# Layer 0 without full-height products: sums by turns and a small product, projection in halves, queries' products moved into layer 1

## Chip, cores and metric

The kernel runs on one NeuronCore of one Trainium2 chip. The metric is the device time of one execution in microseconds. Everything is float32. Before the change, three runs give 3160.32, 3160.87 and 3160.97 us, median 3160.87 us.

## What is computed

The input is x of shape (4, 128, 64, 64): four batches, 128 channels, 4096 positions. Three parts follow one another.

```python
# layer 0, on the group-normalised input
vg = sigmoid(conv_bn(x, Wvg, svg, bvg)); v, gate = split(vg, 2)
q = conv_bn(x, Wq, sq, bq) * 64**-0.5        # 64 channels
k = conv_bn(x, Wk, sk, bk)                   # 64 channels
attn = softmax(einsum('bdn,bdm->bnm', q, k))
out = einsum('bcm,bnm->bcn', v, attn) * gate
x = x + conv_bn(out, Wp, sp, bp)             # the projection
# layer 1, on tokens t = x turned to (batch, position, channel)
h = layernorm(t)
q = einsum('bsd,de->bse', h, W)              # queries are the keys too
t = t + einsum('bst,btd->bsd', softmax(einsum('bsd,btd->bst', q, q)), h)
# a recurrent layer over the positions
Wx = batchnorm(layernorm(t) @ W.T)
t = t + scan(lambda y, wx: sigmoid(wx + y @ V.T), Wx)
```

## The kernel before

**Tiling.** For each batch the kernel runs `layer0` (L368) and then `layer1` (L435). The 4096 positions make 8 blocks of 512 (`QB`, `NB`), each of 4 tiles of 128 (`NQ`).

**Layer 0.** `attention` (L178) takes the blocks in order. For each block it goes through 16 pairs of key tiles. A pair has two scores products (L200), each with a contraction over 64 channels only, one on rows 0 to 63 and one on rows 64 to 127 of the array. They write `ps`, a tile of two PSUM banks from a pool with two buffers (tag "s"). ScalarE takes the exponential of both at once (L202), VectorE adds it to `acc` (L209), which gathers the sums of the softmax for each of the 128 key rows, and two pairs later `weigh` (L376) multiplies it with the values: four products, again each over 64 rows, into two accumulators `o`. When the last pair of a block has been weighed, `finish` (L389) adds the two accumulators, applies the gate to get `og`, and appends six steps to the queue `pending`: `sums`, `projection`, `nothing`, `tokens`, `nothing`, `queries` (L430). The loop takes one step from it at each second pair (L217). The last block's steps are left for layer 1.

**The steps.** `sums` calls `denominators` (L222): VectorE folds the two halves of `acc`, and four products of 128x128 with a column of ones (L227, tile `md`) sum over the key rows, which leaves one sum per position, with the positions on the partitions. `projection` is one 128x128x512 product (L409, tile `mt`), over all 128 rows. `tokens` (L412) scales the projected values, adds the input, stores the tokens and normalises them into `h`. `queries` (L422) is one 128x128x512 product (L424, tile `mq`) that ScalarE copies into `qt` (L427). All three products go to PSUM pool `ps_m`, which has one buffer.

**Turns.** `move` (L235) turns a 128x512 tile from channels on partitions to positions on partitions, or back. VectorE's transpose turns blocks of 32x32 in place (L241), one DMA writes the result to DRAM (L244) and four read it back so that the blocks change places (L246). It is used for the input (in `sums`), for the projected values and for `h`. All DMAs concerned are issued by SP.

**Layer 1.** It takes block 6 first, then 7, then 5 down to 0 (L560). Scores between two blocks serve both: `e` as it is (`direct`, L460), and turned by VectorE (L584) and sixteen DMAs `tt<-dd` (L605) for the other block (`reversed_products`, L471). All products here go over 128 rows. In each step of the inner loop one item of `pending` is taken, or, if it is empty, one of `ahead`, which prepares the next batch (L598 to L601).

**Order.** The program text gives the order in which work is put out. The framework then orders each engine's instructions by what it takes to be ready, so an instruction on VectorE, SP or GpSimd can stand at another place than in the text: the input of a block is loaded and turned during the block before.

Of the kernel before, what the change touches and what calls it, by code (L numbers as in the profile page):

```python
# [18 lines left out]
P = 128  # L19
B, C, N = 4, 128, 4096  # L20
DQ = 64
SCALE = DQ ** -0.5
GROUP = 4
NT = N // P
# [5 lines left out]
QB = 512  # L30
# [18 lines left out]
@with_exitstack  # L49
def conv_attn_hybrid_kernel(  # L50
    ctx: ExitStack,
    tc: tile.TileContext,
    x: bass.AP,
    wts: bass.AP,
    cols: bass.AP,
    rows: bass.AP,
    out: bass.AP,
):
    nc = tc.nc

# [35 lines left out]
    nc.gpsimd.affine_select(  # L96
        out=gview, in_=gview, compare_op=ALU.is_ge, fill=0.0, base=GROUP - 1,
        pattern=[[GROUP, P // GROUP], [0, GROUP]], channel_multiplier=-1,
    )
    mhalf = const.tile([P, NQ], F32, name="mhalf")  # L100
    nc.gpsimd.memset(mhalf, -0.5)
    ones = const.tile([P, 1], F32, name="ones")
    nc.gpsimd.memset(ones, 1.0)
    shift = const.tile([P, 1], F32, name="shift")
    nc.gpsimd.memset(shift, -SHIFT)

    nc.vector.tensor_mul(w_v, w_v, bc[:, 0, :])
    nc.vector.tensor_mul(w_p, w_p, bc[:, 2, :])
    w_vs, w_ps = w_v, w_p

    par2 = const.tile([P, 2], F32, name="par2")
    nc.vector.tensor_scalar(par2, par[:, SG : BG + 1], 0.5, None, ALU.mult)
# [7 lines left out]
    fast(  # L120
        tc, x, out, t_d, t2_d, wxs_d, turn_d,
        dict(qk=w[:, DQ : DQ + P], vs=w_vs, g=w_g, ps=w_ps, a=w_a, f=w_f, vt=v_t),
        col, par, par2, bpc, bc, ident, gavg, ones, shift, inv_sqrt, par_ok,
    )
# [16 lines left out]


def fast(
    tc, x, out, t_d, t2_d, wxs_d, turn_d, wt, col, par, par2, bpc, bc, ident, gavg, ones,
    shift, inv_sqrt, par_ok,
):
    nc = tc.nc
    keep_ctx = ExitStack()
# [4 lines left out]
    with ExitStack() as st:  # L153
# [19 lines left out]
        def flush(until=None):  # L173

            while pending and until not in done:
                pending.popleft()()
# [42 lines left out]
            while fifo:  # L219
                pop()  # L220

        def denominators(acc, at, rinv):  # L222

            nc.vector.tensor_tensor(acc[:, 0, :], acc[:, 0, :], acc[:, 1, :], ALU.add)
            m = ps_m.tile([P, NQ], F32, tag="m", name="md")
            for j in range(NQ):
                nc.tensor.matmul(  # L227
                    m[:, j : j + 1], lhsT=acc[:, 0, bass.ts(j, P)], rhs=ones,
                    start=True, stop=True,
                )  # L230
            den = den_all[:, at : at + NQ]
            nc.vector.tensor_copy(den, m)
            nc.vector.reciprocal(rinv, den)

        def move(blocks, dst):  # L235

# [131 lines left out]
        def layer0(b, gate, q, k, v, need):  # L368
# [20 lines left out]
            def finish(n, o, acc):  # L389
                cs, ts = bass.ts(n, QB), bass.ts(n, NQ)  # L390
                og = work.tile([P, QB], F32, tag="og", name="og")
                nc.scalar.copy(og, o[1])
                nc.vector.tensor_tensor(og, o[0], og, ALU.add)
                nc.vector.tensor_tensor(og, og, gate[:, cs], ALU.mult)
                rinv = stat.tile([P, NQ], F32, tag="rinv", name="rinv")
                xb = work.tile([P, QB], F32, tag="xb", name="xb")
                t = work.tile([P, 4, NQ, 32], F32, tag="t", name="t", bufs=2)
                yt = work.tile([P, 4, NQ, 32], F32, tag="h2", name="yt")
                ht = work.tile([P, 4, NQ, 32], F32, tag="th", name="ht")
                nc.sync.dma_start(xb, x[b, :, cs])  # L400
                nc.gpsimd.tensor_scalar(xb, xb, bpc, None, ALU.add)  # L401

                def sums():
                    denominators(acc, b * NT + n * NQ, rinv)
                    move(xb.rearrange("c (j f k) -> c j f k", j=NQ, f=4), t)

                def projection():
                    m = ps_m.tile([P, QB], F32, tag="m", name="mt")
                    nc.tensor.matmul(m, lhsT=wt["ps"], rhs=og, start=True, stop=True)  # L409
                    move(m.rearrange("c (j f k) -> c j f k", j=NQ, f=4), yt)  # L410

                def tokens():  # L412
                    for j in range(NQ):
                        nc.vector.scalar_tensor_tensor(
                            t[:, :, j, :], yt[:, :, j, :], rinv[:, j : j + 1], t[:, :, j, :],
                            ALU.mult, ALU.add,
                        )
                    nc.sync.dma_start(t_d[b, n], t)
                    layernorm(tiles(t), quarters(h[:, ts, :]))
                    move(h[:, ts, :].rearrange("q j (p i) -> q j p i", p=4), ht)  # L420

                def queries():  # L422
                    m = ps_m.tile([P, QB], F32, tag="m", name="mq")
                    nc.tensor.matmul(  # L424
                        m, lhsT=wt["a"], rhs=ht.rearrange("c f j k -> c j f k"), start=True, stop=True
                    )
                    nc.scalar.copy(qt[:, cs], m)  # L427
                    done.add((b, n))

                pending.extend([sums, projection, nothing, tokens, nothing, queries])  # L430

            attention(score_mm, None, SCALE, weigh, finish, need)
            return h, qt
# [1 line left out]
        def layer1(b, h, qt):  # L435
# [12 lines left out]
            n_turned = 0  # L448
            parts = [0] * NB
            begun = set()  # L450

            def order(n):


                return [0, 1] if b == B - 1 and n == 0 else list(range(n, -1, -1))
# [104 lines left out]
            for n in [NB - 2, NB - 1] + list(range(NB - 3, -1, -1)):  # L560
                o = None
                flush((b, n))
                for a in order(n):
                    if turns(n, a):
                        d = dd[:, n_turned % 2]
# [2 lines left out]
                    for i in range(2):  # L568
# [18 lines left out]
                                )  # L587
                        if o is None:
                            o = ps_o.tile([P, QB], F32, tag="o", name="o")
                        fifo.append((n, a, i, e, o))  # L590
                        clock += 1
                        if len(fifo) > LAG:
# [556 lines left out]
```

## Time and profile before

Stages, from windows of the trace (us of busy time in each window):

| Stage | Window | Length | TensorE | VectorE | ScalarE |
|---|---|---|---|---|---|
| start | 0 to 25.9 | 25.9 | 7.9 | 14.9 | 4.1 |
| batch 0, layer 0 | 25.9 to 408.4 | 382.5 | 382.3 | 222.0 | 152.9 |
| batch 0, layer 1 | 408.4 to 794.6 | 386.2 | 381.2 | 218.7 | 129.3 |
| batch 1, layer 0 | 794.6 to 1162.6 | 368.0 | 368.0 | 214.8 | 140.8 |
| batch 1, layer 1 | 1162.6 to 1548.8 | 386.2 | 381.2 | 218.7 | 129.3 |
| batch 2, layer 0 | 1548.8 to 1916.8 | 368.0 | 368.0 | 214.7 | 140.8 |
| batch 2, layer 1 | 1916.8 to 2303.1 | 386.3 | 381.3 | 218.7 | 129.3 |
| batch 3, layer 0 | 2303.1 to 2671.0 | 367.9 | 367.9 | 214.7 | 140.9 |
| batch 3, layer 1 | 2671.0 to 3040.0 | 369.0 | 360.4 | 182.7 | 112.9 |
| its end, recurrent layer | 3040.0 to 3157.6 | 117.6 | 73.4 | 72.4 | 47.9 |

TensorE is the engine that is hardly ever idle; the others are busy for about a third to three fifths of each attention stage. The groups that the change concerns, from the page and the groups by shape:

| Line | What | Count | Mean of one, ns |
|---|---|---|---|
| L200 | scores, 64x512, TensorE | 2048 records | 602 |
| L383 | weighing, 64x512, TensorE | 4096 records | 589 |
| L227 | sums, 128x1, TensorE | 256 records | 251 |
| L409 | projection, 128x512, TensorE | 64 records | 638 |
| L424 | queries, 128x512, TensorE | 64 records | 639 |
| L202 | exponential, 128x1024, ScalarE | 512 | 1024 |
| L427 | copy of the queries, 128x512, ScalarE | 32 | 586 |
| L209 | accumulation of the sums, 128x1024, VectorE | 448 | 1220 |
| L224 | folding the sums, 128x512, VectorE | 32 | 692 |
| L232 | copy of the sums, 128x4, VectorE | 32 | 162 |
| L241 | turn of 128x512, VectorE | 96 | 702 to 718 |

A matmul in this type leaves two records, and [...]records overlap. What a product costs is read better from the distance between the starts of its neighbours, or from the chain of waits, than from the mean of a record.

### The profile page before, as it was taken

Reading aid. Unit: us, or ns where it says so; the run is one execution under the profiler, and the core shown is the slowest. Engines: PE = TensorE matmul, PEld = TensorE weight load, DVE = VectorE, ACT = ScalarE, POOL = GpSimd, SP = SyncE. Lnnn points to the kernel's source line nnn. Section 1 sums busy time; section 2 is a strip of 40 time slices with the busy share of each in tenths; the row PEclk is TensorE's granted clock in tenths of the full one; section 3 lists DMA queues with packets and bytes.
Section 4 is the critical chain, followed back from the end, with each engine's and each line's share of the span. In section 5 each row is a group of like instructions: output and inputs, shape, how many; then the busy total and the mean of one; then the engine's idle time right before and its main releaser. Section 6 shows DMA issues by size and latency. Waiting matters only on the chain.

```text
span 3157.6 us, 32263 instructions
## 1 busy us (share of the span) xinstructions
PE 3071.5 (97%) x10770; PEld 1374.8 (44%) x10770; DVE 1792.3 (57%) x2964; ACT 1128.2 (36%) x1986; POOL 141.4 (4%) x183
## 2 busy tenths in 40 slices
PE   7999999999999999999999999999999999999976
PEld 3444444444444444444444444444444444444433
DVE  6555556555555555655555555555555655454546
ACT  3433333333333333333333333333333333223324
POOL 0000000000000000000000000000000000000000
PEclk9999999999999999999999999999999999999988
DMA  1111133333111123334211113333321112443324
GB/s 50 37 44 54 54 100 93 92 90 92 48 50 51 54 70 91 96 87 98 70 54 51 54 45 98 93 93 93 88 53 54 54 48 72 136 105 89 98 87 169
DMA packets 233167, 241.14 MB, mean 76 GB/s; under 512 B 88480, under 2 KB 144288, under 8 KB 231968
## 3 DMA queue, kind: packets, MB, share of 16 engines
q1 hardware_dynamic: 231984, 238.18, 27.2%
q8 instruction: 89, 1.46, 0.2%
q10 hardware_dynamic: 1008, 0.79, 0.1%
q14 instruction: 86, 0.70, 0.1%
HBM read 65.80 MB, written 56.62 MB: 39 GB/s over the span
## 4 chain that ended last, share of the span: by engine, by line
PE 91%; DVE 4%; POOL 1%; DMA 1%; SPq 1%; issue 1%; ACT 1%; ACTq 0%; DVEq 0%; POOLq 0%
PE o L383 28%; PE ps L200 15%; PE o L463 14%; PE ps L573 13%; PE ot L476 12%; PE mt L409 1%; PE mq L424 1%; PE mw L544 1%; PE md L227 1%; PE mp L315 1%; PE ps_r L719 1%; PE mh L539 1%; POOL rstd L117 1%; DVE t1b L521 1%; PE mp L350 1%
## 5 line engine op out<-in xcount | busy, mean ns | idle before, releaser
L383 PE MATMUL o<-e,nxt 64*128 64x512 f32 x4096 | 963.8, 589 | 0.0
L202 ACT ACTIVATE e<-ps 128x1024 f32<-128x1024 f32 x512 | 521.2, 1024 | 742.7 <-PE ps L200 738.1
L209 DVE TENSOR_TENSOR acc<-acc,e 128x1024 f32<-128x1024 f32 x448 | 546.4, 1220 | 387.9 <-ACT e L202 376.6
L579 ACT ACTIVATE e<-ps,shift 128x512 f32<-128x512 f32 x580 | 394.0, 684 | 776.4 <-PE ps L573 486.2
L383 PEld LDWEIGHTS o<-e,nxt 64*128 64x128 f32 x4096 | 398.9, 187 | 482.4 <-issue 474.6
L573 PE MATMUL ps<-qt 128*128 128x512 f32 x1160 | 550.4, 595 | 3.0 <-ACT e L579 3.0
L200 PE MATMUL ps<-nxt 64*128 64x512 f32 x2048 | 540.9, 602 | 1.2 <-DVE nxt L327 0.9
L463 PE MATMUL o<-e,h 128*128 128x512 f32 x1160 | 537.0, 592 | 0.0
L476 PE MATMUL ot<-tt,h 128*128 128x512 f32 x888 | 401.5, 595 | 5.3 <-DMA tt<-dd 5.3
L584 DVE STREAM_TRANSPOSE dd<-e 128x512 f32<-128x512 f32 x444 | 286.1, 685 | 110.8 <-ACT e L579 57.3
L463 PEld LDWEIGHTS o<-e,h 128*128 128x128 f32 x1160 | 218.4, 190 | 262.1 <-issue 261.2
L573 PEld LDWEIGHTS ps<-qt 128*128 128x128 f32 x1160 | 213.2, 191 | 244.4 <-issue 224.2
L200 PEld LDWEIGHTS ps<-nxt 64*128 64x128 f32 x2048 | 189.5, 186 | 248.0 <-issue 162.7
L476 PEld LDWEIGHTS ot<-tt,h 128*128 128x128 f32 x888 | 168.3, 191 | 217.1 <-issue 212.4
L481 DVE TENSOR_REDUCE slots<-tt 128x4 f32<-128x2048 f32 x111 | 250.6, 2258 | 11.3 <-DMA tt<-dd 11.2
L490 DVE TENSOR_TENSOR oacc<-oacc,ot 128x512 f32<-128x512 f32 x87 | 59.3, 682 | 209.5 <-PE ot L476 209.5
L116 POOL TENSOR_SCALAR rstd<-mv 128x4 f32<-128x4 f32 x64 | 14.6, 228 | 2519.5 <-DVE mv L257 2519.5
L579 ACT ACTIVATION_READ_ACCUMULATOR e<-ps,shift 128x1 f32 x580 | 113.9, 196 | 0.0
L401 POOL TENSOR_SCALAR xb<-xb,bpc 128x512 f32<-128x512 f32 x32 | 54.3, 1698 | 318.0 <-DMA xb<-in_x_dram 285.2
L117 POOL TENSOR_TENSOR rstd<-rstd,mhalf 128x4 f32<-128x4 f32 x64 | 66.4, 1038 | 5.3
L719 PE MATMUL ps_r<-y,w 128*128 128x256 f32 x168 | 54.4, 443 | 9.8 <-ACT y L716 7.8
L260 DVE TENSOR_SCALAR h<-t,mv,rstd 128x128 f32<-128x128 f32 x128 | 35.7, 343 | 45.3 <-POOL rstd L117 45.3
(124 smaller groups left out, 1411.8 us busy)
## 6 DMA issues: line engine op xcount, KB each, us to landing
tt<-dd SPq DMA_DIRECT2D x1776, 64.0 KB, 2.0
turn_d<-d SPq DMA_DIRECT2D x96, 256.0 KB, 2.0
t_d<-t SPq DMA_DIRECT2D x64, 256.0 KB, 2.0
nxt<-in_x_dram SPq DMA_DIRECT2D x16, 512.0 KB, 5.8
xb<-in_x_dram SPq DMA_DIRECT2D x32, 256.0 KB, 2.9
t<-turn_d SPq DMA_DIRECT2D x128, 64.0 KB, 2.0
yt<-turn_d SPq DMA_DIRECT2D x128, 64.0 KB, 1.9
ht<-turn_d SPq DMA_DIRECT2D x128, 64.0 KB, 2.0
```

The costliest lines, as they stand in the source:

```text
L117: nc.gpsimd.tensor_tensor(dst, dst, mhalf[:, :n], ALU.pow)
L200: nc.tensor.matmul(ps[:, h, :], lhsT=lhsT, rhs=rhs, start=True, stop=True)
L202: nc.scalar.activation(e, ps, AF.Exp, scale=scale)
L209: nc.vector.tensor_tensor(acc, acc, e, ALU.add)
L383: nc.tensor.matmul(o[r], lhsT=v[rs, p + h * PAIRS, :], rhs=e[rs, h, :], start=(p == 0 and h == 0), stop=(p == PAIRS - 1 and h == 1),)
L463: nc.tensor.matmul(o, lhsT=h[:, NQ * a + 2 * i + half, :], rhs=e[:, half, :], start=(a == order(n)[0] and i == 0 and half == 0), stop=(a = ...
L476: nc.tensor.matmul(ot, lhsT=h[:, NQ * n + j, :], rhs=t[:, :, j, :, :].rearrange("q p k j -> q k p j"), start=(j == 0), stop=(j == NQ - 1),)
L481: nc.vector.tensor_reduce(slots[:, bass.ts(n, NQ), a], t.rearrange("q p b k j -> q b p (k j)"), AX.XY, ALU.add,)
L573: nc.tensor.matmul(ps[:, half, :], lhsT=qt[:, bass.ts(at, P)], rhs=qt[:, bass.ts(n, QB)], start=True, stop=True,)
L579: nc.scalar.activation(e[:, half, :], ps[:, half, :], AF.Exp, bias=shift, accum_out=slots[:, at, n : n + 1],)
L584: nc.vector.transpose(d.rearrange("q f b k j -> q k b f j")[:, 2 * i + half], e[:, half, :].rearrange("q (b f j) -> q b f j", b=NQ, f=NQ),)
L719: nc.tensor.matmul(bank(k, s), lhsT=wt["vt"], rhs=before, start=False, stop=True, skip_group_check=True,)
```

## The change

The denominators, the projection and the queries of layer 0 are computed in another way or at another place; the result is meant to be the same.

- **Sums.** `sums` still folds the halves of `acc`, but then VectorE turns the 32x32 blocks of the folded half into the other half of `acc` and adds up each row of a block (512 to 16 columns, tile `sub`). A new step `denominators` multiplies `sub` with a constant matrix `quart`, in two products of 64 rows each (`halves`), which adds the four groups of 32 partitions. VectorE then adds the two partial results, keeps for each partition the column of its own group (`own`, a mask) and adds that up.
- **Projection.** One product over 128 rows becomes two over 64 rows each, through the same `halves`. ScalarE copies one partial result, VectorE adds the other, and the turn reads the sum from SBUF.
- **Buffers.** `halves` takes its PSUM tile from the pool of the scores (tag "s", two buffers), not from `ps_m`.
- **Queries.** `tokens` now turns `h` straight into its place in `qt`, and the block counts as done there. The product is made in layer 1, in the pass of block 6: for block 6 ahead of the first scores, for block a-1 in the first half of key block a, for block 7 in the last half of key block 0. The result replaces the turned `h` in `qt`.
- **Queue.** The six steps are `sums`, `nothing`, `denominators`, `projection`, `nothing`, `tokens`.
- Two small constants, `quart` and `own`, are built at the start by VectorE.

```diff
+        def halves(lhsT, rhs):
+            cols = rhs.shape[-1]
+            m = ps_s.tile([P, 2, QB], F32, tag="s", name="m2")
+            for r in range(2):
+                rs = bass.ts(r, DQ)
+                nc.tensor.matmul(m[:, r, :cols], lhsT=lhsT[rs], rhs=rhs[rs], start=True, stop=True)
+            return m[:, 0, :cols], m[:, 1, :cols]
...
                 def sums():
-                    denominators(acc, b * NT + n * NQ, rinv)
+                    half, blocks = acc[:, 0, :], acc[:, 1, :]
+                    nc.vector.tensor_tensor(half, half, blocks, ALU.add)
+                    nc.vector.transpose(blocks, half)
+                    nc.vector.tensor_reduce(
+                        sub, blocks.rearrange("q (j f k) -> q j f k", j=NQ, f=4), AX.X, ALU.add
+                    )
                     move(xb.rearrange("c (j f k) -> c j f k", j=NQ, f=4), t)
 
+                def denominators():
+                    m0, m1 = halves(quart, sub.rearrange("q j f -> q (j f)"))
+                    tot = stat.tile([P, NQ, 4], F32, tag="tot", name="tot", bufs=2)
+                    flat = tot.rearrange("q j f -> q (j f)")
+                    nc.vector.tensor_copy(flat, m0)
+                    nc.vector.tensor_tensor(flat, flat, m1, ALU.add)
+                    nc.vector.tensor_tensor(
+                        tot, tot,
+                        own.rearrange("q (j f) -> q j f", j=1).to_broadcast([P, NQ, 4]), ALU.mult,
+                    )
+                    den = den_all[:, b * NT + n * NQ : b * NT + (n + 1) * NQ]
+                    nc.vector.tensor_reduce(den, tot, AX.X, ALU.add)
+                    nc.vector.reciprocal(rinv, den)
+
                 def projection():
-                    m = ps_m.tile([P, QB], F32, tag="m", name="mt")
-                    nc.tensor.matmul(m, lhsT=wt["ps"], rhs=og, start=True, stop=True)
-                    move(m.rearrange("c (j f k) -> c j f k", j=NQ, f=4), yt)
+                    m0, m1 = halves(wt["ps"], og)
+                    nc.scalar.copy(og, m1)
+                    nc.vector.tensor_tensor(og, m0, og, ALU.add)
+                    move(og.rearrange("c (j f k) -> c j f k", j=NQ, f=4), yt)
...
-                    move(h[:, ts, :].rearrange("q j (p i) -> q j p i", p=4), ht)
-
-                def queries():
-                    m = ps_m.tile([P, QB], F32, tag="m", name="mq")
-                    nc.tensor.matmul(
-                        m, lhsT=wt["a"], rhs=ht.rearrange("c f j k -> c j f k"), start=True, stop=True
+                    move(
+                        h[:, ts, :].rearrange("q j (p i) -> q j p i", p=4),
+                        qt[:, cs].rearrange("c (p j k) -> c p j k", j=NQ, p=4),
                     )
-                    nc.scalar.copy(qt[:, cs], m)
                     done.add((b, n))
 
-                pending.extend([sums, projection, nothing, tokens, nothing, queries])
+                pending.extend([sums, nothing, denominators, projection, nothing, tokens])
...
+            def queries(n):
+                cs = bass.ts(n, QB)
+                m = ps_m.tile([P, QB], F32, tag="m", name="mq")
+                moved = qt[:, cs].rearrange("c (p j k) -> c j p k", j=NQ, p=4)
+                nc.tensor.matmul(m, lhsT=wt["a"], rhs=moved, start=True, stop=True)
+                nc.scalar.copy(qt[:, cs], m)
...
                 flush((b, n))
+                if n == NB - 2:
+                    queries(n)
                 for a in order(n):
...
+                        if n == NB - 2 and i == 0 and a > 0:
+                            queries(a - 1)
+                        elif n == NB - 2 and a == 0 and i == 1:
+                            flush((b, NB - 1))
+                            queries(NB - 1)
                         fifo.append((n, a, i, e, o))
```

More of the change, by code (lines that the diff above doesn't have):

```diff
@@ L99, in conv_attn_hybrid_kernel @@
     )
+    quart = const.tile([P, P], F32, name="quart")
+    nc.vector.tensor_tensor(
+        quart.rearrange("p (a i) -> p a i", a=4),
+        ident[:, 0:32].rearrange("p (a i) -> p a i", a=1).to_broadcast([P, 4, 32]),
+        ident[:, 32:64].rearrange("p (a i) -> p a i", a=1).to_broadcast([P, 4, 32]), ALU.add,
+    )
+    for i in range(2, 4):
+        nc.vector.tensor_tensor(
+            quart.rearrange("p (a i) -> p a i", a=4), quart.rearrange("p (a i) -> p a i", a=4),
+            ident[:, 32 * i : 32 * i + 32].rearrange("p (a i) -> p a i", a=1).to_broadcast([P, 4, 32]),
+            ALU.add,
+        )
+    own = const.tile([P, 4], F32, name="own")
+    nc.vector.tensor_reduce(own, ident.rearrange("p (a i) -> p a i", a=4), AX.X, ALU.add)
     mhalf = const.tile([P, NQ], F32, name="mhalf")
@@ L122, in conv_attn_hybrid_kernel @@
         dict(qk=w[:, DQ : DQ + P], vs=w_vs, g=w_g, ps=w_ps, a=w_a, f=w_f, vt=v_t),
-        col, par, par2, bpc, bc, ident, gavg, ones, shift, inv_sqrt, par_ok,
+        col, par, par2, bpc, bc, ident, gavg, quart, own, shift, inv_sqrt, par_ok,
     )
@@ L143, in fast @@
 def fast(
-    tc, x, out, t_d, t2_d, wxs_d, turn_d, wt, col, par, par2, bpc, bc, ident, gavg, ones,
-    shift, inv_sqrt, par_ok,
+    tc, x, out, t_d, t2_d, wxs_d, turn_d, wt, col, par, par2, bpc, bc, ident, gavg, quart,
+    own, shift, inv_sqrt, par_ok,
 ):
@@ L220, in attention @@
                 pop()
[L222 to L233, printed above, removed]
+        def halves(lhsT, rhs):
[5 more added lines that the diff above has]
+            return m[:, 0, :cols], m[:, 1, :cols]
         def move(blocks, dst):
@@ L398, in finish @@
                 yt = work.tile([P, 4, NQ, 32], F32, tag="h2", name="yt")
-                ht = work.tile([P, 4, NQ, 32], F32, tag="th", name="ht")
                 nc.sync.dma_start(xb, x[b, :, cs])
                 nc.gpsimd.tensor_scalar(xb, xb, bpc, None, ALU.add)
+                sub = stat.tile([P, NQ, 4], F32, tag="sub", name="sub", bufs=2)
                 def sums():
-                    denominators(acc, b * NT + n * NQ, rinv)
-                    move(xb.rearrange("c (j f k) -> c j f k", j=NQ, f=4), t)
+                    half, blocks = acc[:, 0, :], acc[:, 1, :]
[3 more added lines that the diff above has]
+                        sub, blocks.rearrange("q (j f k) -> q j f k", j=NQ, f=4), AX.X, ALU.add
+                    )
+                    move(xb.rearrange("c (j f k) -> c j f k", j=NQ, f=4), t)
+                def denominators():
[4 more added lines that the diff above has]
+                    nc.vector.tensor_tensor(flat, flat, m1, ALU.add)
+                    nc.vector.tensor_tensor(
+                        tot, tot,
+                        own.rearrange("q (j f) -> q j f", j=1).to_broadcast([P, NQ, 4]), ALU.mult,
+                    )
+                    den = den_all[:, b * NT + n * NQ : b * NT + (n + 1) * NQ]
+                    nc.vector.tensor_reduce(den, tot, AX.X, ALU.add)
+                    nc.vector.reciprocal(rinv, den)
                 def projection():
-                    m = ps_m.tile([P, QB], F32, tag="m", name="mt")
-                    nc.tensor.matmul(m, lhsT=wt["ps"], rhs=og, start=True, stop=True)
-                    move(m.rearrange("c (j f k) -> c j f k", j=NQ, f=4), yt)
+                    m0, m1 = halves(wt["ps"], og)
+                    nc.scalar.copy(og, m1)
+                    nc.vector.tensor_tensor(og, m0, og, ALU.add)
+                    move(og.rearrange("c (j f k) -> c j f k", j=NQ, f=4), yt)
                 def tokens():
@@ L419, in tokens @@
                     layernorm(tiles(t), quarters(h[:, ts, :]))
-                    move(h[:, ts, :].rearrange("q j (p i) -> q j p i", p=4), ht)
-                def queries():
-                    m = ps_m.tile([P, QB], F32, tag="m", name="mq")
-                    nc.tensor.matmul(
-                        m, lhsT=wt["a"], rhs=ht.rearrange("c f j k -> c j f k"), start=True, stop=True
+                    move(
+                        h[:, ts, :].rearrange("q j (p i) -> q j p i", p=4),
+                        qt[:, cs].rearrange("c (p j k) -> c p j k", j=NQ, p=4),
                     )
-                    nc.scalar.copy(qt[:, cs], m)
                     done.add((b, n))
-                pending.extend([sums, projection, nothing, tokens, nothing, queries])
+                pending.extend([sums, nothing, denominators, projection, nothing, tokens])
             attention(score_mm, None, SCALE, weigh, finish, need)
```

## Prediction

> **What bounds the kernel now.** I read three views in this order: the page's engine shares, the chain of waits inside one block of layer 0, and the chain at the start of layer 1. The page first.
>
> ```profile
> PE 3071.5 (97%) x10770; PEld 1374.8 (44%) x10770; DVE 1792.3 (57%) x2964; ACT 1128.2 (36%) x1986; POOL 141.4 (4%) x183
> ...
> PE 91%; DVE 4%; POOL 1%; DMA 1%; SPq 1%; issue 1%; ACT 1%; ACTq 0%; DVEq 0%; POOLq 0%
> ```
>
> TensorE is busy 97% of the span and carries 91% of the chain that ended last, so what is taken off its row comes off the time, as long as nothing else steps into the gap. Next the chain between 1020 and 1072 us, inside layer 0 of batch 1. Columns: start, length, what, number of records (a matmul of this type leaves two records).
>
> ```profile
> 1022.79 1.72 PE o L383 x8
> 1024.51 0.86 PE ps L200 x4
> 1025.37 3.43 PE o L383 x16
> 1028.80 0.98 PE md L227 x8
> 1029.78 1.92 PE ps L200 x8
> 1031.70 1.72 PE o L383 x8
> 1033.42 1.06 PE mt L409 x2
> 1034.47 1.06 PE ps L200 x4
> 1035.53 1.72 PE o L383 x8
> ...
> 1053.56 1.72 PE o L383 x8
> 1055.27 1.06 PE mq L424 x2
> 1056.33 1.06 PE ps L200 x4
> 1057.39 1.72 PE o L383 x8
> ```
>
> There is no gap. A pair of key tiles costs 0.86 (scores) + 1.72 (weighing) = 2.575 us, and a block has 16, 41.2 us. The block takes 44.895 us (the same place of the next blocks is 44.89 or 44.90 us later in the whole chain), so three additions make 3.70 us: the sums md, the projection mt and the queries mq. Each makes the scores behind it longer too: 1.06 instead of 0.86, and 1.92 instead of 1.72. So mt and mq cost 1.06 + 0.20 = 1.26 each, md 0.98 + 0.20 = 1.18; together 3.70. That closes exactly. Last the same products at the start of layer 1 (1162 to 1200 us), among others of full height.
>
> ```profile
> 1162.63 1.91 PE ps L573 x4
> 1164.55 0.79 PE md L227 x8
> 1165.33 1.82 PE ps L573 x4
> 1167.15 0.86 PE mt L409 x2
> 1168.01 1.72 PE ps L573 x4
> ...
> 1192.05 0.86 PE ps L573 x2
> 1192.90 0.86 PE mq L424 x2
> 1193.76 0.86 PE ps L573 x2
> ```
>
> The same mq costs 0.86 us there and leaves its neighbours alone. The 0.40 us on top in layer 0 is the price of going from half-height to full-height products and back.
>
> **The skill.** "TensorEngine Tiling (Array Packing)", Key Properties: changing the tiling mode drains TensorE, changing only the tile does not. The trace agrees and prices it: 0.40 us for the two changes; ps to o, both of half height, change weights and destination at no visible cost. "TensorE: Matmul & The Clock Gate", The mechanism: products on different row groups run side by side. The trace agrees: the two halves (64x512 each) of a scores product take 0.86 us for four records, what one 128x512 takes. Same page, LDWEIGHTS: a load's time follows its columns, not its rows. The trace agrees: 186 ns for 64x128, 191 for 128x128; I use this for the small product.
>
> **The change, part by part.** All sums are against the profiled span, 3157.6 us; the timed runs lie at 3160.32 to 3160.97, some 3.3 higher, so I take the difference off their median, 3160.87. Of the 32 blocks, 28 finish inside layer 0 (blocks 0 to 6 of four batches) and 4 (block 7) at the start of layer 1.
>
> *Removed in layer 0:* md, mt, mq: 3.70 us a block.
>
> *Projection in halves:* two 64x512 products side by side without a mode change, 0.86 us, by the scores row. ScalarE gets a copy (0.586, the row of og<-o), VectorE an addition (0.67); the turn that follows (0.72) is there before too.
>
> *Sums:* on TensorE two 64x128 loads, each passed twice, with 16 columns moving. Nothing in the trace is like it. From below: two passes at md's pitch, 0.97 us for 8 loads = 0.12, so 0.2 us if both halves load side by side and nothing else shows. From above: four loads in a row and an uncovered load before the scores, 0.55. I take 0.35. On VectorE: one more turn (0.70), a 512-column reduction (estimate 0.69, by the 692 ns addition of that width; the 2048-column one takes 2258), three operations more on 4 to 16 columns (0.16 each, by the 162 ns copy of md); with the projection's addition 2.5 us a block. VectorE is busy 25.9 of 44.9 us in a block, so 28.4 of 42.4 after. What hides it: about 1.35 us of waiting for ScalarE behind each accumulation, and the 3.97 us in which VectorE waits for md at 1029.8, whose place the turn and the reduction take. Cost nothing; if not, the slower rival below.
>
> *Queries in layer 1:* 0.86 us each, by the mq row there. 28 x 0.86 = 24.1 us comes back. Their copies (0.586) go before later scores: the one for block a-1 is issued a whole key block ahead, with a second scores product (1.72) and usually a weighing between, so hidden. The one for block 6 is not: it is the first thing in layer 1, and the first scores need it. Last weighing ends, product, copy 0.59 plus about 0.15 of hand-over: TensorE stands about 0.75 us, bounds 0 (if it is issued earlier) and 2.
>
> *Block 7's steps stay in layer 1*, now with half-height products there: 0.35 + 0.86 + two times 0.40, against 0.79 + 0.10 + 0.86 before: +0.26 us.
>
> *DMAs:* each block still has three turns, of one DMA out and four back; the last four now land in qt instead of ht. None is added. In layer 0 the tokens step is popped at pair 10 instead of 6. Before, it took 11.6 us from its first VectorE operation (1040.7) to the landed turn (ht's last issue ends at 1050.3, and a landing takes 2.0: 1052.3). Block 6's now begins with 5 pairs and two weighings to go, 16.3 us: in time. Block 7's comes two steps later in layer 1, some 7 us, in the SP queue that carries tt<-dd; before, ht was issued at 1187.4, and qt is needed when the second block starts, near 1226.7. Hidden, but with less to spare.
>
> *Setup:* four small VectorE operations while x loads; nothing.
>
> *The sum:* 28 x (3.70 - 0.86 - 0.35) = 69.7 off; 24.1 + 4 x 0.75 + 4 x 0.26 = 28.1 on. Net 41.6: 3157.6 to 3116.0 in the profile, **3119 us** timed. The small product's bounds move it by -4 and +6, the start of layer 1 by -3 and +5.
>
> **The rivals.** *A, as above, 0.62:* 3110 to 3128.
>
> *B, the turns at the start of layer 1 come late, 0.20.* Against: 39 us between ht's issue and the need before. For: SP then issues tt<-dd without a break, 51 us for 73 of them, 0.7 each, and one set of sixteen ahead of the turn is 11 us; in the last batch the loads of wxs hold one turn for 13.6 us already, and TensorE waits 5.3 us for tt<-dd there. A wait of 2 to 7 us in each of four layers gives 3127 to 3147; middle 3137.
>
> *C, the change doesn't do what it says, 0.06:* if a pair of halves between other halves still paid 0.40, two of them would give back 28 x 0.80 = 22.4: 3142. Against: 0.86 + 1.72 with no surcharge at each turn from ps to o.
>
> *D, the scores' buffer becomes the bound, slower, 0.08.* The new products take one of the two buffers of ps. The scores two pairs on need it 0.86 + 1.72 = 2.58 us after the product ends; copy and addition free it after some 1.5, the small reads after 0.7. If VectorE does the next accumulation first (exp 1.02, accumulation 1.22), it comes free near 3.9 and 3.5 us, and TensorE stands 1.3 + 1.0 us a block: 28 x 2.3 = 64 on, 3183. It decides from 48 us, 0.86 us for each of 56 products. Against: the reads are issued ahead of that accumulation, and VectorE has caught up by pair 4.
>
> The remaining 0.04 is B and C together, within 0.2%.
>
> **Range and chances.** A and most of B make 8 in 10: 3108 to 3138, the low end being the small product at 0.2 and no stand, with 4 us for what I can't see. 0.2% is 6.3 us, about what a measurement of this kernel can tell from no change. Faster: A, B, C, 0.88; same 0.04; slower D, 0.08.
>
> **What would show it.** In the chain of a layer 0 block: 42.4 us between blocks instead of 44.9, no scores at 1.06, m2 for the projection at 0.86, for the sums at 0.2 to 0.55. In layer 1: mq at 0.86 without neighbours lengthened, and one gap under 1 us at its start. Layer 0 gets some 17.4 us shorter a batch, layer 1 some 7.0 longer. Wrong: TensorE waits on m2's readers (D), on qt's turn (B), or a surcharge on half-height neighbours (C).

## The result, and the profile after

The changed kernel takes 3107.61 us (median of 4 runs, 3107.13 to 3108.91), the kernel before 3160.85 (4 runs, 3160.32 to 3160.97). The ratio is 0.9833, with a 95% interval of 0.9816 to 0.985: 53.2 us or 1.7% less. The prediction said 3119, faster; the measured time lies 0.4 us below the low end of its range, which is less than the spread of the four runs (1.8). Two profiled executions differ by a little less, 3157.6 against 3106.2 us of span, 51.4 us.

From the page of the changed kernel, engine shares and the chain that ended last:

```profile
PE 3018.6 (97%) x10706; PEld 1362.3 (44%) x10706; DVE 1877.7 (60%) x3160; ACT 1144.8 (37%) x2018; POOL 144.5 (5%) x183
...
PE 91%; DVE 4%; SPq 1%; POOL 1%; DMA 1%; issue 1%; ACT 0%; ACTq 0%; DVEq 0%; POOLq 0%
```

TensorE is as full as before, with 52.9 us less of busy time. VectorE has 85.4 us more and still stands at 60%: this work was added beside the path.

The chain of waits inside a block of layer 0 of batch 1 (start, length, what, records; L215 are the scores, L394 the weighing, L243 the two products in halves):

```profile
1004.64 3.43 PE o L394 x16
1008.07 1.72 PE ps L215 x8
1009.79 1.72 PE o L394 x8
...
1014.94 1.72 PE o L394 x8
1016.66 0.13 PE m L243 x4
1016.78 0.95 PE ps L215 x4
1017.74 1.72 PE o L394 x8
...
1020.31 1.72 PE o L394 x8
1022.03 0.86 PE m L243 x4
1022.89 0.86 PE ps L215 x4
1023.75 1.72 PE o L394 x8
```

The scores are 0.86 on both sides of the projection, and the projection itself is 0.86: a product in halves among other halves pays nothing on top. The weight loads of the two kernels show where the surcharge sits. First the kernel before, around its projection (L409), then the changed kernel (start, length, PEld is TensorE's weight load; "issue" in the last bracket: the profile shows nothing that it waited for):

```profile
1032.39 0.19 PEld L383 LDWEIGHTS o<-e,nxt 64*128 64x128 f32 x2 [0.24 <-issue]
1033.35 0.30 PEld L409 LDWEIGHTS mt<-og,w 128*128 128x128 f32 x2 [0.76 <-issue]
1034.40 0.30 PEld L200 LDWEIGHTS ps<-nxt 64*128 64x128 f32 x4 [0.76 <-issue]
```

```profile
1021.43 0.19 PEld L243 LDWEIGHTS m<-og,w 64*128 64x128 f32 x2 [0.23 <-ACT e L217]
1021.86 0.19 PEld L243 LDWEIGHTS m<-og,w 64*128 64x128 f32 x2 [0.23 <-issue]
```

In the changed kernel a load starts every 0.43 us, one record ahead of its product: the projection's first product starts at 1021.86, its load at 1021.43. At a change of height in the kernel before, the load starts only with its own product, at 1033.35, 0.96 after the load ahead of it. So the 0.20 us for one change is about one weight load (0.19) that nothing covers. That is a reading of the trace; no run tests why the load isn't put ahead.

The sums take 0.13, and the scores behind them 0.95 instead of 0.86: 0.22 us together, where md took 1.18. No scores at 1.06 are left. The block is 3.70 - 0.86 - 0.22 = 2.62 us shorter, which is 18.3 us for the seven blocks of a layer 0. In the prediction's view of layer 1 the three old products cost 0.89, 0.86 and 0.86, in layer 0 1.18, 1.26 and 1.26. So 7 x 1.09 = 7.6 of the 18.3 us are the changes of height, 7 x 0.86 = 6.0 are the queries, which come back in layer 1, and 7 x (0.89 - 0.22) = 4.7 are the sums, whose new product is cheaper by itself.

The chain at the start of layer 1 of the same batch (L487 are the queries, L613 the scores):

```profile
1134.06 1.07 PE mq L487 x2
1135.13 0.02 issue
1135.15 0.59 ACT qt L488
1135.75 0.04 issue
1135.79 1.98 PE ps L613 x4
1137.77 0.86 PE mq L487 x2
1138.63 3.43 PE ps L613 x8
1142.07 0.86 PE mq L487 x2
1142.92 1.72 PE o L501 x4
1144.64 0.33 PE m L243 x4
1144.97 1.91 PE ps L613 x4
...
1148.60 1.06 PE m L243 x4
```

Here is the one stand of TensorE (time in which it does nothing) that the prediction named: ScalarE's copy of block 6's queries. The waits of TensorE give its size in all four layers, and show which wait is gone (the first line is of the kernel after, "us in total, times, longest us"):

```profile
PE ps L613 <- ACT qt L488: 2.7, 4, 0.7
```

In the kernel before, the same list had a wait that the one after does not have:

```profile
PE ot L476 <- DMA tt<-dd: 5.3, 3, 3.0
```

Where the time went, by stage. A stage begins with its first scores, or with the queries' product ahead of them; all numbers are from the starts of TensorE's records, in us. "Layer 0" and "layer 1" are those of batch 1 (batch 2's are within 0.5 of them, but for the layer 1 of the kernel with the start filled, 393.7); "last layer 1" runs to the first product of the recurrent steps with y, so it takes in the preparation for them.

| Kernel | Timed | Layer 0 | Layer 1 | Last layer 1 |
|---|---|---|---|---|
| before | 3160.85 | 368.0 | 386.2 | 402.6 |
| changed | 3107.61 | 349.7 | 392.8 | 401.7 |
| sums alone | 3134.46 | 361.3 | 385.7 | 404.3 |
| queries alone | 3131.97 | 359.2 | 388.7 | 401.9 |
| projection alone | 3149.78 | 365.3 | 386.1 | 403.0 |
| full height, grouped | 3142.34 | 363.6 | 386.1 | 402.3 |
| full height, other pool | 3191.16 | 368.0 | 393.0 | 412.8 |
| changed, slot held | 3122.11 | 351.9 | 392.8 | 402.0 |
| changed, start filled | 3105.95 | 349.7 | 392.0 | 401.1 |
| changed, four steps | 3102.53 | 349.7 | 390.1 | 403.6 |
| changed, block 7 full | 3104.28 | 349.7 | 391.0 | 403.3 |
| changed, block 7 full, four steps | 3097.23 | 349.7 | 388.7 | 403.9 |
| the same, start filled | 3094.44 | 349.7 | 388.0 | 402.8 |

For the change: four layers 0 at 18.3 off make 73.2; three layers 1 at 6.6 on make 19.8; the last layer 1 gives 0.9 more; the start takes 1.4 longer and the recurrent end, which is 84.0 to 87.0 in these kernels, 1.4. That is 51.5, the difference of the two spans.

### The profile page after: what moved, and what is told of

Read it like the earlier page. It is cut to its first block, busy times and chain, and to the rows that moved or that the text cites. A ratio compares the mean times of both kernels' runs of the same rounds, so it can differ in the third digit from the quotient of the medians.

```text
span 3106.2 us, 32252 instructions
## 1 busy us (share of the span) xinstructions
PE 3018.6 (97%) x10706; PEld 1362.3 (44%) x10706; DVE 1877.7 (60%) x3160; ACT 1144.8 (37%) x2018; POOL 144.5 (5%) x183
## 4 chain that ended last, share of the span: by engine, by line
PE 91%; DVE 4%; SPq 1%; POOL 1%; DMA 1%; issue 1%; ACT 0%; ACTq 0%; DVEq 0%; POOLq 0%
PE o L394 28%; PE ps L215 15%; PE ps L613 15%; PE o L501 14%; PE ot L514 12%; SPq L650 1%; PE m L243 1%; PE mw L582 1%; PE mq L487 1%; PE mp L326 1%; PE ps_r L764 1%; PE mh L577 1%; POOL rstd L132 1%; DVE t1b L559 1%; PE mp L361 1%; PE mp L346 1%
## 5 line engine op out<-in xcount | busy, mean ns | idle before, releaser
L394 PE MATMUL o<-e,nxt 64*128 64x512 f32 x4096 | 963.8, 589 | 0.0
L394 PEld LDWEIGHTS o<-e,nxt 64*128 64x128 f32 x4096 | 399.0, 187 | 482.3 <-issue 474.5
L613 PE MATMUL ps<-qt 128*128 128x512 f32 x1160 | 547.8, 595 | 2.7 <-ACT qt L488 2.7
L215 PE MATMUL ps<-nxt 64*128 64x512 f32 x2048 | 534.5, 596 | 1.2 <-DVE nxt L338 0.9
L613 PEld LDWEIGHTS ps<-qt 128*128 128x128 f32 x1160 | 213.4, 191 | 249.0 <-issue 224.2
L215 PEld LDWEIGHTS ps<-nxt 64*128 64x128 f32 x2048 | 194.5, 187 | 231.5 <-issue 158.8
L448 DVE SCALAR_TENSOR_TENSOR t<-yt,rinv,t 128x128 f32<-128x128 f32 x128 | 36.6, 347 | 71.5 <-DMA yt<-turn_d 71.4
```

The source lines that it names most:

```text
L215: nc.tensor.matmul(ps[:, h, :], lhsT=lhsT, rhs=rhs, start=True, stop=True)
L394: nc.tensor.matmul(o[r], lhsT=v[rs, p + h * PAIRS, :], rhs=e[rs, h, :], start=(p == 0 and h == 0), stop=(p == PAIRS - 1 and h == 1),)
L613: nc.tensor.matmul(ps[:, half, :], lhsT=qt[:, bass.ts(at, P)], rhs=qt[:, bass.ts(n, QB)], start=True, stop=True,)
```

## The experiments

**Theories.** M: a full-height product among half-height ones pays 0.40 us for two changes of height, and the gain of layer 0 is these changes, the products that leave it and the cheaper sums. P: the 0.40 comes from the single buffer of the PSUM pool that md, mt and mq shared. Two more questions came up on the way: what holding a slot of the scores' pool costs, and what sets the length of layer 1.

**The sums alone.** The kernel before with the new `sums` and `denominators`; projection and queries as they were.

```diff
-                pending.extend([sums, projection, nothing, tokens, nothing, queries])
+                pending.extend([sums, nothing, denominators, projection, nothing, tokens, nothing, queries])
...
```

> Of the change only the sums: folded, turned and reduced by VectorE, then the small product in halves; projection and queries as before. Theory M (a full-height product among half-height ones pays 0.40 us for two changes of height): 28 blocks lose md's 1.18 us and gain the small product at 0.22 (from the trace after), 26.9 us; block 7's four gain 0.3 each; 3133 us. Rival P (the price is in the single buffer of the PSUM pool that these products use, not in the height): the same, since the sums leave that pool too. If the sums' VectorE steps matter: over 3140.

Measured: 3134.46 us (ratio 0.9914, 0.9897 to 0.993). Layer 0 is 6.7 us shorter, which is 7 x (1.18 - 0.22) = 6.7. VectorE's additional steps cost nothing that shows.

**The queries alone.** The kernel before with the queries' products in layer 1.

```diff
-                    move(h[:, ts, :].rearrange("q j (p i) -> q j p i", p=4), ht)
...
+                    move(
+                        h[:, ts, :].rearrange("q j (p i) -> q j p i", p=4),
+                        qt[:, cs].rearrange("c (p j k) -> c p j k", j=NQ, p=4),
...
-                pending.extend([sums, projection, nothing, tokens, nothing, queries])
+                pending.extend([sums, projection, nothing, tokens])
...
+                if n == NB - 2:
+                    queries(n)
...
+                        if n == NB - 2 and i == 0 and a > 0:
+                            queries(a - 1)
...
```

> Of the change only the queries' products moved into layer 1. Theory M: 28 times 0.40 us saved, the product itself (0.86) only changes place, and TensorE stands 0.68 us at the start of each layer 1: 11.2 - 2.7 = 8.5 us, 3152 us. Rival P: no gain, since the product keeps its pool and its copy: 3161 to 3164. If the 5.3 us of TensorE waiting for the turned tiles in the last layer 1 go with the queries: 3147.

Measured: 3131.97 us (0.9908, 0.9892 to 0.9925), 20 us below what M said. M holds in layer 0: 8.8 us off, 7 x 1.26. Layer 0 alone doesn't part M from P, since the products have left it. Layer 1 speaks against P: pool and copy are the same, and a product of the queries takes 0.86 there, not 1.26. What was wrong is the length of layer 1. Seven products of 0.86 and a stand of 0.68 should lengthen it by 6.7; it is 2.5 longer, and the last one 0.7 shorter. Windows over layer 1 of batch 1, first before, then this kernel (window; length; busy time and count of TensorE, its weight loads, VectorE, ScalarE and GpSimd; clock, DMA share, GB/s):

```profile
1162.60:1548.80 386.20, 381.19 (x990) 173.22 (x988) 218.72 (x376) 129.28 (x326) 9.68 (x16) 1.00 0.39 98
```

```profile
1147.40:1536.10 388.70, 385.75 (x1004) 176.41 (x1002) 218.26 (x376) 132.72 (x333) 9.67 (x16) 1.00 0.38 96
```

Fourteen records more raise the busy time by 4.6, and the idle time falls from 5.0 to 2.9 us, the new stand included. So part of the products fell into time in which TensorE had waited. The waits that are no longer there are those of its scores for ScalarE (0.75 and 0.25 us) and of the next batch's preparation for VectorE (0.30) at the second block, one of 0.65 ahead of a turn of h, and 0.7 of the 0.95 ahead of the last such turn. These and the new stand make 2.1 of the 4.2 us that the sum was off; the rest shows in no wait of the list. How the order of the steps moves such waits is taken up with the last experiments.

**The projection alone.** The kernel before with the projection in halves.

```diff
-                    m = ps_m.tile([P, QB], F32, tag="m", name="mt")
-                    nc.tensor.matmul(m, lhsT=wt["ps"], rhs=og, start=True, stop=True)
-                    move(m.rearrange("c (j f k) -> c j f k", j=NQ, f=4), yt)
+                    m0, m1 = halves(wt["ps"], og)
+                    nc.scalar.copy(og, m1)
+                    nc.vector.tensor_tensor(og, m0, og, ALU.add)
+                    move(og.rearrange("c (j f k) -> c j f k", j=NQ, f=4), yt)
```

> Of the change only the projection in two halves, with its result in the scores' pool; sums and queries as before. Theory M: 28 times 0.40 us saved in layer 0, that is 2.8 us less in each layer 0; layer 1 pays 0.40 for block 7 and may move by 1 to 4 us with the order of its steps: 3151 us. If half-height products cost what full-height ones do, changes included: 3160.

Measured: 3149.78 us (0.9968, 0.9957 to 0.9979). Layer 0 is 2.7 us shorter; M said 2.8. The three parts make 6.7 + 8.8 + 2.7 = 18.2 us in a layer 0, and the whole change 18.3. They add up there.

**Full height, but grouped.** The kernel before, where sums, projection and the block before's queries come in one step, so that TensorE changes height once for the three.

```diff
-                def sums():
-                    denominators(acc, b * NT + n * NQ, rinv)
-                    move(xb.rearrange("c (j f k) -> c j f k", j=NQ, f=4), t)
+                def products():
+                    denominators(acc, b * NT + n * NQ, rinv)
+                    pair = ps_s.tile([P, 2, QB], F32, tag="s", name="mt")
+                    nc.tensor.matmul(pair[:, 0, :], lhsT=wt["ps"], rhs=og, start=True, stop=True)
+                    while held:
+                        held.popleft()(pair[:, 1, :])
...
-                pending.extend([sums, projection, nothing, tokens, nothing, queries])
+                pending.extend([nothing, products, nothing, tokens])
+                if n >= NB - 2:
+                    pending.extend([nothing, queries])
```

> The kernel before with the same products at full height, but next to one another: the sums and the projection of a block and the queries of the block before it in one step (projection and queries write the two banks of one tile of the scores' pool); block 6's queries alone, block 7's steps in layer 1. Theory M: 13 pairs of changes fewer in each batch, 52 times 0.40 = 20.8 us: 3140 us. A theory in which half-height products are themselves cheaper: no change, 3161.

Measured: 3142.34 us (0.9945, 0.9928 to 0.9961), 18.0 us less where M said 20.8, and with the very products of before. This is the plainest proof that the height changes cost time: no product was taken away. The results of projection and queries also go to another pool here; the next kernel shows that this alone leaves layer 0 as it was. Its chain in a block shows where the rest of M's figure stayed:

```profile
1023.01 1.72 PE o L384 x8
1024.73 0.98 PE md L227 x8
1025.71 0.97 PE mt L407 x2
1026.68 0.86 PE mt L429 x2
1027.54 1.06 PE ps L200 x4
```

The three with the longer scores behind them take 0.98 + 0.97 + 0.86 + 0.20 = 3.01 us, against 3.70 apart: 0.69 saved and not 0.80, because the projection right behind md takes 0.97 and not 0.86. Full-height scores behind md are longer by the same 0.10 in layer 1, where no height changes, so this part was never a price of the change: md's own surcharge is 0.29, and 0.40 holds for a long product that stands alone.

**Full height, other pool.** The kernel before, with the results of projection and queries in the scores' pool.

```diff
-                    m = ps_m.tile([P, QB], F32, tag="m", name="mt")
+                    m = ps_s.tile([P, 2, QB], F32, tag="s", name="mt")[:, 0, :]
...
-                    m = ps_m.tile([P, QB], F32, tag="m", name="mq")
+                    m = ps_s.tile([P, 2, QB], F32, tag="s", name="mq")[:, 0, :]
```

> The kernel before with the projection's and the queries' results in the scores' PSUM pool (two buffers) instead of the pool with one buffer; heights and order as before. Theory M: no change, 3160 to 3162 us. Rival P: the extra 0.40 us of both goes, 28 blocks and two products, 22 us: 3138 us.

Measured: 3191.16 us (1.0098, 1.0082 to 1.0115), 31 us slower. Layer 0 is 368.0 as before, so P falls for both products. But M's "no change" for the whole kernel was wrong as well: the three layers 1 are 6.5 to 6.9 longer, the last 10.1. There block 7's mq takes a slot of the scores ahead of its turned operand. TensorE in the timeline of that kernel, in layer 1 of batch 1 and, in the last line, of the last batch (last bracket: idle time before it, and what ended it):

```profile
1192.77 0.38 PE L302 MATMUL gv<-gdev,gavg 128*128 128x1 f32 x2 [0.70 <-DVE gdev L296]
1194.97 1.12 PE L315 MATMUL mp<-nxt,w 128*128 128x512 f32 x2 [1.81 <-DVE nxt L308]
1198.81 2.08 PE L315 MATMUL mp<-nxt,w 128*128 128x512 f32 x2 [2.72 <-DVE nxt L327]
1200.68 1.92 PE L424 MATMUL mq<-ht,w 128*128 128x512 f32 x2
1202.38 4.40 PE L573 MATMUL ps<-qt 128*128 128x512 f32 x8
...
2730.29 2.04 PE L424 MATMUL mq<-ht,w 128*128 128x512 f32 x2 [16.29 <-DMA ht<-turn_d]
```

In the kernel before, mq stood between scores that went on (1192.05 to 1193.76 in the prediction's view). Here the scores stand behind it. In batch 1 the operand landed at 1197.70, and ahead of mq TensorE did only the next batch's preparation, with 0.70 + 1.81 + 2.72 = 5.2 us of waits; in the last batch, with nothing to prepare, it stood 16.3 us. That the scores can't pass because their slot is given out after mq's fits this order, and wasn't tested apart.

Waiting was not all. Behind these waits the granted clock of TensorE stood at 0.50, from 1197.2 to 1204.0 and from 2716.1 to 2733.2: mq's two records take 1.92 us where they take 1.02 in the timeline before, and the first eight of the scores 4.40 where eight take 3.60 at the full clock. In batch 1 the listed idle time grew by 4.7 us; the other 2.1 of the 6.8 us fit this clock. The kernel's mean granted clock was 0.987, against 0.993 before.

**The slot held longer.** The changed kernel with six multiplications by one ahead of the projection's addition.

```diff
                     nc.scalar.copy(og, m1)
+                    for _ in range(6):
+                        nc.vector.tensor_scalar(og, og, 1.0, 0.0, ALU.mult, ALU.add)
                     nc.vector.tensor_tensor(og, m0, og, ALU.add)
```

> The changed kernel with six 128x512 multiplications by one on VectorE between the projection's copy and its addition, so that the scores' PSUM slot of each projection is kept some 2.6 to 3.4 us longer (0.43 to 0.57 each); the result is the same. In the trace after, that slot is free 1.35 us after the product and needed 2.58 us after it, 1.23 us to spare. If the slot is what would bound: TensorE stands 1.4 to 2.2 us in each of 28 blocks, 39 to 62 us on 3107.6, some 3147 to 3170. If VectorE's time alone matters, whose load stays under the block's length: 3108 to 3111.

Measured: 3122.11 us (0.9878, 0.9862 to 0.9895), 14.5 more than the changed kernel, where the slot theory had said 39 to 62. The block's TensorE and VectorE, from the two timelines:

```profile
1029.06 1.03 PE L243 MATMUL m<-og,w 64*128 64x512 f32 x4
1029.91 1.02 PE L215 MATMUL ps<-nxt 64*128 64x512 f32 x4
1030.77 1.88 PE L394 MATMUL o<-e,nxt 64*128 64x512 f32 x8
1032.49 1.02 PE L215 MATMUL ps<-nxt 64*128 64x512 f32 x4
1033.35 1.88 PE L394 MATMUL o<-e,nxt 64*128 64x512 f32 x8
1035.27 1.13 PE L215 MATMUL ps<-nxt 64*128 64x512 f32 x4
```

```profile
1030.74 2.73 DVE L444 TENSOR_SCALAR og<-og 128x512 f32<-128x512 f32 x6 [0.91 <-ACT og L442]
1033.39 1.22 DVE L224 TENSOR_TENSOR acc<-acc,e 128x1024 f32<-128x1024 f32 x1
1034.53 0.69 DVE L445 TENSOR_TENSOR og<-m,og 128x512 f32<-128x512 f32 x1
```

The addition frees the slot at 1035.22, 5.3 us after the product. The second scores behind the product, at 1032.49, did not wait for it; the third, at 1035.27, did, 0.20 us, and the weighing behind it came 0.10 late. So the slot is needed some 5.15 us after the product (1035.07), not 2.58, as if the other buffer served two scores in a row. Seven blocks at 0.3 make 2.1 of the 2.2 us by which layer 0 of batch 1 is longer. VectorE moved an accumulation ahead of the addition, just as rival D feared, and it cost 0.3 us and not 1.3. Batch 0's layer 0 is 6.0 us longer: besides the same 2.1, its scores at 149.68 waited 1.94 us for ScalarE, and behind this wait the granted clock was 0.50 from 150.1 to 153.5, while TensorE worked all the time, some 1.7 us lost.

**What sets the length of layer 1.** Four kernels on the changed one. First, block 5's queries right behind block 6's, so that TensorE works while ScalarE copies:

```diff
...
                 if n == NB - 2:
                     queries(n)
+                    queries(n - 1, ps_s.tile([P, 2, QB], F32, tag="s", name="mq5")[:, 0, :])
...
-                        if n == NB - 2 and i == 0 and a > 0:
+                        if n == NB - 2 and i == 0 and 0 < a < n:
```

> The changed kernel with block 5's queries issued right behind block 6's at the start of layer 1, into a slot of the scores' pool, so that TensorE has work while ScalarE copies block 6's queries. If the stand of 0.68 us per layer is all that the start costs: 4 x 0.68 = 2.7 us less, 3105 us. If the slot is missed by the scores: no gain or a loss.

Measured: 3105.95 us (0.9826, 0.9809 to 0.9842; 4 runs of 3104.26 to 3107.18). The stand is gone, and two layers 1 are 0.7 and 0.8 shorter, the third 0.9 longer. In the third, which has the same waits as the other two, the granted clock was 0.50 from 1962.1 to 1965.5 with TensorE at work; that is 1.7 us, the whole difference. By the time alone the gain is at the edge of the runs' spread.

Second, four steps for block 7 instead of six, so that the next batch's preparation, which comes only when no step is pending, begins two inner steps earlier:

```diff
-                pending.extend([sums, nothing, denominators, projection, nothing, tokens])
+                if n == NB - 1:
+                    pending.extend([sums, denominators, projection, tokens])
+                else:
+                    pending.extend([sums, nothing, denominators, projection, nothing, tokens])
```

> The changed kernel with four steps instead of six for block 7 (sums, denominators, projection, tokens), whose steps run in layer 1, one per inner step, ahead of the next batch's preparation. The queries-only kernel has four there, and its layer 1 takes 388.7 us, the changed kernel's 392.8. Theory S (the empty steps push the preparation to a worse place): layer 1 near 389, 12 us less in three layers, 3096 us. Theory H (block 7's half-height products in layer 1 are what costs): no change, 3107 us.

Measured: 3102.53 us (0.9814, 0.9798 to 0.9831), layer 1 at 390.1, 2.7 shorter. Third, block 7 with its sums and projection at full height, in the `ps_m` pool, in six steps (sums, projection, nothing, tokens, nothing, nothing):

```diff
...
                 def projection():
+                    if n == NB - 1:
+                        m = ps_m.tile([P, QB], F32, tag="m", name="mt")
+                        nc.tensor.matmul(m, lhsT=wt["ps"], rhs=og, start=True, stop=True)
+                        move(m.rearrange("c (j f k) -> c j f k", j=NQ, f=4), yt)
+                        return
...
```

> The changed kernel with block 7's sums and projection at full height, as before the change, and still six steps for it. Theory H (half-height products in layer 1 cost 4.1 us a layer): layer 1 near 389, 3095 us. Theory S (the number of steps counts): layer 1 stays at 392.8, 3107 us.

Measured: 3104.28 us (0.9821, 0.9804 to 0.9837), layer 1 at 391.0, 1.8 shorter. Neither theory explains the 4.1 us alone, and this edit moved the steps as well as the height: the tokens are the fourth step here and the sixth in the changed kernel. Then both together, four steps at full height, which gives layer 1 the steps of the queries-only kernel:

```diff
-                    pending.extend([sums, projection, nothing, tokens, nothing, nothing])
+                    pending.extend([sums, projection, nothing, tokens])
```

> The changed kernel with block 7's sums and projection at full height and four steps for it (sums, projection, nothing, tokens), so that its layer 1 is that of the queries-only kernel, while layer 0 stays as changed. If the order of the steps makes layer 1's length: 388.7 us a layer as in that kernel, 4.1 less than changed in three layers, 3095 us. If the two parts found so far (1.7 for the height, 2.7 for the number of steps) are one and the same thing: 390 a layer, 3100 us.

Measured: 3097.23 us (5 runs, 3095.52 to 3098.19; 0.9799, 0.9785 to 0.9812). Layer 1 is 388.7 us, as in the queries-only kernel, and layer 0 349.7 as in the changed one. With the start filled too:

> The same with block 5's queries right behind block 6's at the start of layer 1, in a slot of the scores' pool. If the gains add up: 0.7 us less in each layer 1 than the kernel without it, 3092 to 3098 us. If the slot makes the scores wait: no gain.

Measured: 3094.44 us (5 runs, 3093.88 to 3095.21; 0.9792, 0.9779 to 0.9806), layer 1 at 388.0. This is the fastest of all, 66 us under the kernel before; against the changed kernel, by the two medians and not side by side, 13 us. What is shown is that the same work takes 388.0 to 392.8 us in layer 1 by the form, place and number of block 7's steps and by what fills the start. The waits of TensorE in layer 1 of batch 1 show what each edit takes away. In the changed kernel they are 5.9 us; besides the stand there are the turns of h, 3.7 us, and the next batch's preparation:

```profile
PE mp L326 <- DVE nxt L351: 0.8, 1, 0.8
PE mp L346 <- DVE nxt L351: 0.8, 1, 0.8
```

With four steps one of these two remains, and the turns of h wait for 2.2 us; with block 7 at full height both are gone, and the turns wait for 3.6; with both edits the preparation doesn't wait and the turns wait for 2.2; with the start filled the stand is gone too. In sum the waits are 5.9, 3.9, 4.3, 2.9 and 2.3 us. Block 7's half-height products themselves are not the cost: they take 1.77 us in the chain against 1.75 before. Up to 1.2 us of the differences in length shows in no wait of the list and stays open, and so does why a step at one place makes VectorE late at another.

## Why the prediction was right, and where its terms were off

**The main step stood.** That TensorE's row is the time, that the surcharge in layer 0 is 0.40 us for two changes of height around a long product, and that layer 0 gives back the difference: the grouped kernel shows it without removing a product, and the three single parts add up to 18.2 of 18.3 us. The Trainium skill, "TensorEngine Tiling (Array Packing)", Key Properties, says that changing the tiling mode drains TensorE; the trace agrees in so far as going there and back costs 0.40 us around a lone full-height product of 512 columns. The predicted 17.4 us per layer 0 was 18.3.

**The small product** was taken at 0.35 with 0.2 as its lower end. It is 0.22: 28 x 0.13 = 3.6 us of the 11.6 that were missed. The lower bound, two load passes at md's pitch, was nearly the cost.

**Layer 1** was to be 7.0 us longer in all four batches. Three are 6.6 longer (1.2 us of the miss): there the term was right in size and in kind, as TensorE's waits are 5.9 us against 5.0 before, the stand of 0.7 included. The last is 0.9 shorter instead, 7.9 us of the miss. The step that failed is "28 x 0.86 = 24.1 us comes back": for the last layer 1 it took the products to be added to a row without gaps. There TensorE had waited 5.3 us for tt<-dd, which the prediction quoted under rival B as a danger and not as room. The longest of these waits in the kernel before, with the same product a little earlier beside it:

```profile
2733.46 3.60 PE L476 MATMUL ot<-tt,h 128*128 128x512 f32 x8
...
2743.44 5.14 PE L476 MATMUL ot<-tt,h 128*128 128x512 f32 x8 [2.96 <-DMA tt<-dd]
```

The eight records behind the wait take 5.14 us instead of 3.60, which fits the granted clock, 0.50 from 2743.0 to 2746.4. In the changed kernel neither is there: TensorE's idle time in the last layer 1 falls from 16.8 to 12.0 us, the new stand included, and the clock gives back some 1.5; together 6.3 of the 7.9, the rest stays open. The waits for tt<-dd are there with the sums or the projection alone (6.7 and 4.3 us) and none, or at most 1.8 us, in the kernels that move the queries. Against that, the start, put at no cost, and the recurrent end took 1.4 us more each; and 1.8 us is that the profiled runs lie closer together than the medians. So more than half of the miss is luck in the last batch, and not a better price of the change. In the kernel with the queries alone and in the last two, where block 7 has other steps, the seven products lengthen a whole layer 1 by 2.5 us or less; in the changed kernel they do not.

**The stand at the start** was put at 0.75 and is 0.68; block 7's half-height products at +0.26, and the chain gives 0.33 + 1.06 with 0.38 on the scores behind, 1.77 in all against 0.79 + 0.10 + 0.86 = 1.75: as good as nothing.

**Rivals.** B did not come: the last turns into qt were issued at 1167.0 to 1169.0 and no product waited for them. C falls by the 0.86 beside 0.86. D is real and was wrongly priced: a held slot does stop the scores, but from 5.15 us after the product and not from 2.58, so with 1.35 us in the changed kernel there were some 3.8 us to spare. A kin of it, a slot taken by a product whose operand is late, fits what made the other-pool kernel slower in layer 1.

## What to carry to other kernels

Look for lone products of another height in a stream, and price each by the distance between its neighbours' starts, not by its record; if they can't be turned into halves, putting them side by side saves more than half of the surcharge (0.69 of 1.09 us here). When work is moved into a stage, count that stage's idle time as possible room, and try the order of the small steps there, which with the filled start was worth 13 us here, as much as the smallest part of the change (11). A product in the pool of the main stream should have its operand ready when its turn comes. And read the granted clock behind a wait before putting a lengthening down to something else: 3.4 us at 0.50 cost some 1.5 to 1.7 us here, as much as the effects that were looked for.

## What the runs showed that I had not expected

Two half-height products with 64x128 weights and 16 columns cost 0.22 us, scores behind them included, where four full-height ones with one column cost 1.18. A PSUM pool of two buffers let the scores run two pairs past a held slot: the wait began only at the third scores, 5.15 us after the product. The same layer 1 was 386.2 us long or 393.0 by nothing but the pool of two products, and with the queries in it 388.0 to 392.8 by small steps. And a row that is 97% busy had 3.4 us at half the clock around the end of a wait of 1.9 us, and of one of 3.0. How long a wait has to be for that, these runs don't say: two waits of 0.8 close together had it behind them in one layer 1 of the kernel with the start filled, and not in the two other layers 1 with the same waits.
